# Weighting gathered pixels with one broadcast product on VectorE after the scan

## The chip, the cores and the metric

The kernel runs on one core of one Trainium2 chip. The metric is the device time of one execution in microseconds. A core has five engines that run their own instruction queues in order and meet through semaphores: TensorE (PE), VectorE (DVE), ScalarE (ACT), GpSimd (POOL) and SyncE (SP). Sixteen DMA engines move data for all queues.

## The reference

The input x has 4 images of 96 channels and 64 x 64 pixels. Four layers follow each other, each added to its input. Layer 0 is a selective scan in four directions over 4096 pixels, with 192 channels of 16 states. Layer 1 is a deformable convolution, and the change is in it:

```python
offset = _conv(x, offset_w, offset_b)
mask = jax.nn.sigmoid(_conv(x, mask_w, mask_b))
...
for k in range(K * K):                       # nine taps
    py = base_y[None, :, None] + i * DIL + dy
    px = base_x[None, None, :] + j * DIL + dx
    samp = _bilinear(x, py, px) * mask[:, k][:, None]
    out = out + jnp.einsum('bchw,oc->bohw', samp, weight[:, :, i, j])
...
# _bilinear: the four pixels around (py, px), weighted
return (1 - wy_) * (1 - wx_) * v00 + (1 - wy_) * wx_ * v01 + wy_ * (1 - wx_) * v10 + wy_ * wx_ * v11
```

Each output pixel thus needs, for each of nine taps, four neighbouring pixels of 96 channels, each times one number, summed. Layer 2 is a spectral filter over the 4096 pixels (a Fourier transform, an elementwise complex step, the inverse) and a feed-forward net with quantised operands; layer 3 is linear attention and a second such net.

## The kernel before, in words

All matrices are spread over 128 partitions. The program is one long list of instructions whose order is made when the kernel is built: nothing is decided on the chip. Layer 0's scan (`Layer0.scan`) runs from near the start until about 7635 us. Two other streams of work are woven into it and go on behind it. The stream `ends` prepares layer 0's inputs for all images and then computes layers 2 and 3 of image 0, 1, 2, 3, one after the other; image b waits until `net.sampled` holds b. The stream `middle` finishes layer 0 for an image, and then does layer 1 for it (`Layer1.image`), image after image.

Both streams are Python generators that yield planned costs. `Clock` keeps, for PE, DVE, ACT and POOL, when each would be free by these costs, and a step is emitted when the engines that it needs are planned to be free within some microseconds (`AHEAD`) and its data are ready. `pipe` keeps several chains of a kind in flight (eight for the sampling), limited by the buffers that they take. A yield's `cost(dve=..., act=...)` is such a plan: it says where the instructions stand in each engine's queue, not how long they take. Once the scan is over, `alone` steps the two streams in turn, and `net.own_banks` is set: the PSUM banks that the scan had are then given to `ends`.

Layer 1 of an image first writes a table in DRAM, in which one row holds a pixel and its three neighbours, 4 x 96 numbers. `positions` computes for every output pixel and tap a row number (`idx`) and four weights with the mask in them (`wt`, 128 partitions x 288 x 4). `sample` then works on blocks of 128 output pixels, t = 0 to 31, and three taps at a time (k0 = 0, 3, 6): 96 triples for an image. For a triple, `taps` does this:

- L1301: three indirect DMAs issued by POOL gather 128 rows each into the tile `g`, 128 x 3 x 384; six such tiles are in turn.
- L1312: twelve ACT activations multiply each group of 96 channels by its weight, one number per partition.
- L1318 and L1319, where `added` holds (`net.own_banks` is set): DVE sums the four corners to one in two adds of 128 x 576 and 128 x 288.
- L1331: PE transposes what is left into PSUM, three matmuls in that case and twelve that accumulate otherwise; L1339: ACT copies to the tile `st`.
- After six triples (two blocks of 128 pixels), L1347: nine matmuls of the convolution, and L1352: DVE adds bias and residual, SP stores (L1354).

In the layers 2 and 3 of the other stream the lines named later are these: L1466 and L1474 the first layer and its scaling on DVE, L1425 with the ACT copy L1434 the transforms by 64, L1491 with the activation L1492 the transform with twiddles, L1505, L1507, L1510 and L1512 the way back with the sum on DVE, L471, L487, L512 the norms, L1637 and L1639 the attention's products.

`added` is true for the sampling of image 3 alone: images 0 to 2 are sampled while the scan runs.

Of the kernel before, what the change touches and what calls it, by code (L numbers as in the profile page):

```python
# [19 lines left out]
B, C, H, W = 4, 96, 64, 64  # L20
# [163 lines left out]
def cost(pe=0.0, dve=0.0, act=0.0, pool=0.0, **more):  # L184
    return Step((pe, dve, act, pool), **more)


def wait(us=0.0, **more):

    return Step((0.0,) * 4, us, **more)  # L190
# [82 lines left out]
def pipe(net, chains, width, every=0, **tiles):  # L273


    chains, active = iter(chains), []
    clock, known, more = net.clock, net.known, True
    end, free = clock.now(), tiles
    while True:
        if more and len(active) < width:  # L280
            steps = next(chains, None)
            if steps is None:
                more = False
            else:
                active.append(Chain(steps, clock.now()))
                continue
        if not active:
            break
        for n, chain in enumerate(active):
            if chain.new and not net.has_bank():  # L290
                continue
            if any(a.done <= chain.done + every for a in active[:n]):
                continue
            if not all(free[tag] > 0 for tag in chain.takes):
                continue
            if clock.has_room(known.get((chain.kind, chain.done), (1.0,) * 4), chain.ready):
                break
        else:
            yield BLOCKED
            continue  # L300
        for tag in chain.takes:
            free[tag] -= 1
        clock.precede(known.get((chain.kind, chain.done), (0.0,) * 4))
        step = next(chain.steps, None)
        if step is None:
            net.hold(-chain.holds)
            active.remove(chain)
            end = max(end, chain.ready)
            continue
        for tag in step.frees:  # L310
            free[tag] += 1
        known[chain.kind, chain.done] = step.work
        chain.ready = clock.queue(step, chain.ready)
        chain.done += 1
        net.hold(step.holds - chain.holds)
        chain.holds, chain.new, chain.takes = step.holds, step.new, step.takes
        yield None
    yield wait(max(0.0, end - clock.now()))
# [796 lines left out]
class Layer1:  # L1115
# [168 lines left out]
    def sample(self, b, idx, wt):  # L1284
        net = self.net
        tc, nc = net.tc, net.nc
        with tc.tile_pool(name=f"l1g{b}", bufs=1, side="right") as gp:
            wdc = gp.tile([C, 9, 128], F32, name=f"wdc{b}", tag="wdc")
            nc.sync.dma_start(wdc, net.ins["wdc"])
            sts = {}  # L1290

            def taps(t, k0):

                yield wait(takes="g")
                key = f"{b}_{t}_{k0}"
                j, q = divmod(t, 2)
                cs = slice(j * 256, (j + 1) * 256)
                g = gp.tile([128, 3, 4 * C], F32, name=f"g{key}", tag="g", bufs=6)
                for k in range(3):
                    n = 9 * t + k0 + k  # L1300
                    nc.gpsimd.indirect_dma_start(  # L1301
                        out=g[:, k, :],
                        out_offset=None,
                        in_=self.tables[b % 2],
                        in_offset=bass.IndirectOffsetOnAxis(ap=idx[:, n : n + 1], axis=0),
                    )
                    yield cost(pool=1.5, wait=7.0 * (k == 2))
                for k in range(3):
                    for c in range(4):
                        pixel = g[:, k, c * C : (c + 1) * C]  # L1310
                        n = 9 * t + k0 + k
                        nc.scalar.activation(pixel, pixel, AF.Identity, scale=wt[:, n, c : c + 1])  # L1312
                    if k < 2:
                        yield cost(act=0.7)
                added = net.own_banks is not None
                if added:

                    nc.vector.tensor_add(g[:, :, : 2 * C], g[:, :, : 2 * C], g[:, :, 2 * C :])  # L1318
                    nc.vector.tensor_add(g[:, :, :C], g[:, :, :C], g[:, :, C : 2 * C])  # L1319
                first = q == 0 and k0 == 0  # L1320
                yield cost(dve=1.0 * added, act=0.7, new=True, takes="st" if first else "")
                if first:
                    sts[j] = gp.tile([C, 9, 256], F32, name=f"st{b}_{j}", tag="st")
                st = sts[j]


                corners = 1 if added else 4
                pt = net.mm(f"ps{key}", C)[:, : 3 * 128].rearrange("p (k t) -> p k t", t=128)
                for k in range(3):
                    for c in range(corners):  # L1330
                        nc.tensor.matmul(  # L1331
                            pt[:, k, :],
                            lhsT=g[:, k, c * C : (c + 1) * C],
                            rhs=net.ident,
                            is_transpose=True,
                            start=(c == 0),
                            stop=(c == corners - 1),
                        )
                nc.scalar.copy(st[:, k0 : k0 + 3, 128 * q : 128 * q + 128], pt)  # L1339
                yield cost(pe=0.4 if added else 1.3, act=0.5, new=True, frees="g")  # L1340
                if q == 0 or k0 < 6:
                    return
                xr = gp.tile([C, 256], F32, name=f"xr1_{b}_{j}", tag="xr")
                nc.sync.dma_start(xr, self.x1[b][:, cs])
                po = net.mm(f"pd{b}_{j}")[:, :256]
                for k in range(9):
                    nc.tensor.matmul(po, lhsT=wdc[:, k, :], rhs=st[:, k, :], start=(k == 0), stop=(k == 8))  # L1347
                    if k % 3 == 2:
                        last = k == 8
                        yield cost(pe=1.4, holds=1, takes="xo" if last else "", frees="st" if last else "")  # L1350
                xo = gp.tile([C, 256], F32, name=f"xo1_{b}_{j}", tag="xo")
                nc.vector.scalar_tensor_tensor(xo, po[:C], net.vec(V_L1B, C), xr, ALU.add, ALU.add)  # L1352
                yield cost(dve=0.5)
                nc.sync.dma_start(self.x2[b][:, cs], xo)  # L1354
                yield wait(frees="xo")

            chains = (taps(t, k0) for t in range(4 * NCH) for k0 in (0, 3, 6))
            yield from pipe(self.net, chains, 8, g=6, st=1, xo=1)

# [429 lines left out]
```

## Time and profile before

| what | value |
|---|---|
| time, median of three runs | 9014.61 us (9012.24 to 9038.34) |
| span of the profiled execution | 8965.3 us |
| median less that span, what lies around it | 49.3 us |
| busy: PE, DVE, ACT, POOL | 6639.1, 6689.3, 5244.1, 5561.5 us |
| activations at L1312 | 4608, of which 1152 for image 3 |
| adds at L1318 | 96, from 7867.9 to 8423.1 us |

The page gives the profiled execution's span, from its first to its last instruction, and no time around it; the runs' times include what lies before and after, so the two differ by the third row. Busy times overlap, since the engines work side by side. A group's line gives its source line, engine, operation, the tiles written and read and their shapes, the count, busy time in us and mean duration in ns, and then how long the engine was idle just before, with what ended the idling. Where the instructions of one group overlap, the busy time is less than the count times the mean. A wait's line says who waited for whom, for how long in total, how often, and the longest.

### The profile page before, as it was taken

How to read it: one execution, taken by the hardware profiler on the slowest of the kernel's cores; microseconds unless marked ns; L12 is line 12 of the kernel's file. 1: busy time of each engine (PE TensorE's matmuls, PEld its weight loads, DVE VectorE, ACT ScalarE, POOL GpSimd, SP SyncE). 2: the span in 40 equal slices, each digit the busy share in tenths (PEclk: the TensorE clock that was granted, in tenths of full speed). 3: DMA queues.
4: the chain of work that ended last, by engine and by line, in shares of the span. 5: the costliest groups of instructions: out<-in, count | busy, mean ns of one | idle time of the engine just before them, and what ended most of it. 6: DMA issues, size and time to landing. Idle time of an engine off the chain costs nothing.

```text
span 8965.3 us, 97776 instructions
## 1 busy us (share of the span) xinstructions
PE 6639.1 (74%) x31960; PEld 2926.8 (33%) x31960; DVE 6689.3 (75%) x4995; ACT 5244.1 (58%) x10214; POOL 5561.5 (62%) x4307
## 2 busy tenths in 40 slices
PE   6675967687767678777667888776888777766687
PEld 2111311122222233312223554122455322454373
DVE  0498889987889987788898887898887889223414
ACT  4564656555567767755566665545666665267623
POOL 0365657666668888766688887667888876245200
PEclk8776977798778889877778888787898887867798
DMA  1476777767778888877788888667888876434120
GB/s 51 133 205 173 193 191 220 198 183 181 189 202 231 235 224 228 204 199 194 200 230 219 233 218 213 160 177 193 215 229 222 216 188 156 104 108 131 57 62 12
DMA packets 776001, 1608.49 MB, mean 179 GB/s; under 512 B 247810, under 2 KB 339358, under 8 KB 773383
## 3 DMA queue, kind: packets, MB, share of 16 engines
q10 hardware_dynamic: 244224, 843.17, 36.4%
q1 hardware_dynamic: 457542, 532.51, 22.0%
q0 software_dynamic: 73728, 226.57, 9.6%
q8 instruction: 257, 4.21, 0.2%
q14 instruction: 250, 2.04, 0.1%
HBM read 1345.62 MB, written 256.29 MB: 179 GB/s over the span
## 4 chain that ended last, share of the span: by engine, by line
PE 35%; DVE 27%; DMA 15%; ACT 10%; issue 7%; POOL 2%; SPq 2%; ACTq 1%; another core or an unknown queue 0%; DVEq 0%; POOLq 0%
DVE hh L960 13%; DVE db L952 7%; DMA du<-du 5%; PE pc L691 4%; PE py L988 4%; ACT g L1312 4%; PE ps L1331 3%; PE db L938 3%; PE f L1425 3%; DMA da<-de 2%; PE pd L1347 2%; POOL hh L969 1%; DMA bc<-bcd 1%; ACT da L932 1%; PE h L1466 1%
## 5 line engine op out<-in xcount | busy, mean ns | idle before, releaser
L969 POOL TENSOR_TENSOR hh<-hh,bc 128x1024 f32<-128x1024 f32 x1536 | 3658.6, 2384 | 351.9 <-DVE hh L960 244.2
L960 DVE TENSOR_TENSOR_SCAN hh<-da,st,db 128x1024 f32<-128x1024 f32 x1152 | 2701.1, 2345 | 229.9 <-PE py L988 86.1
L952 DVE TENSOR_TENSOR db<-db,bc 128x1024 f32<-128x1024 f32 x1536 | 1863.4, 1213 | 523.2 <-PE db L938 517.9
L932 ACT ACTIVATE da<-da,w_al 128x1024 f32<-128x1024 f32 x1536 | 1741.5, 1146 | 641.0 <-DMA da<-de 287.2
L938 PE MATMUL db<-du,rep 96*128 96x512 bf16 x3072 | 1101.2, 447 | 824.6 <-DVE hh L960 764.5
L1301 POOL DMA_INDIRECT g<-table,idx x1152 | 1151.2, 999 | 546.3 <-issue 195.7
L1312 ACT ACTIVATE g<-g,wt 128x96 f32<-128x96 f32 x4608 | 1282.6, 365 | 146.8 <-DMA du<-du 37.3
L988 PE MATMUL py<-hh,w_fold 128*32 128x512 f32 x6144 | 1055.2, 760 | 24.2 <-POOL hh L969 10.7
L960 DVE TENSOR_TENSOR_SCAN hh<-da,db 128x1024 f32<-128x1024 f32 x384 | 877.3, 2285 | 71.9 <-PE py L988 22.1
L1331 PE MATMUL ps<-w_ident,g 128*96 128x128 f32 x3744 | 682.8, 322 | 300.6 <-ACT g L1312 142.7
L938 PEld LDWEIGHTS <-rep 96*128 96x128 bf16 x3072 | 284.3, 107 | 1772.3 <-issue 1139.0
L780 POOL TENSOR_TENSOR lw<-lw,w 128x512 f32<-128x512 f32 x192 | 244.3, 1273 | 820.9 <-DVE w L778 808.7
L1331 PEld LDWEIGHTS ps<-w_ident,g 128*96 128x96 f32 x3744 | 483.2, 142 | 655.0 <-ACT g L1312 255.2
L967 POOL COPY st<-hh 128x1 f32<-128x1 f32 x1152 | 233.3, 202 | 696.0 <-DVE hh L960 637.4
L691 PE MATMUL pc<-pad,wc 96*128 96x512 f32 x1152 | 548.4, 616 | 53.4 <-DMA wc<-wc_d 46.8
L1339 ACT COPY st<-ps 96x384 f32<-96x384 f32 x384 | 180.2, 472 | 395.5 <-PE ps L1331 301.6
L801 PE MATMUL pr<-ex,w_ident 128*128 128x512 f32 x384 | 281.5, 823 | 173.0 <-DVE ex L791 89.8
L778 DVE SCALAR_TENSOR_TENSOR w<-w,ex 128x512 f32<-128x512 f32 x192 | 159.4, 830 | 285.7 <-ACT w L775 285.6
L1318 DVE TENSOR_TENSOR g<-g 128x576 f32<-128x576 f32 x96 | 72.9, 759 | 390.0 <-ACT g L1312 360.5
L691 PEld LDWEIGHTS pc<-pad,wc 96*128 96x128 f32 x1152 | 217.1, 195 | 336.4 <-issue 305.3
L988 PEld LDWEIGHTS py<-hh,w_fold 128*32 128x32 f32 x6144 | 153.9, 122 | 511.0 <-issue 384.4
L769 PE MATMUL pd<-xd,w_dtw 103*64 103x512 f32 (+1 forms) x512 | 267.1, 800 | 66.5 <-DVE rl L782 27.5
(249 smaller groups left out, 8899.5 us busy)
## 6 DMA issues: line engine op xcount, KB each, us to landing
da<-de ACTq DMA_DIRECT2D x1536, 512.0 KB
du<-du SPq DMA_DIRECT2D x512, 192.0 KB
bc<-bcd SPq DMA_DIRECT2D x128, 512.0 KB
du<-du SPq DMA_DIRECT2D x128, 384.0 KB
y<-yb SPq DMA_DIRECT2D x384, 128.0 KB
de<-rl SPq DMA_DIRECT2D x128, 256.0 KB
m<-in_dft SPq DMA_DIRECT2D x128, 256.0 KB
ad<-y ACTq DMA_DIRECT2D x192, 128.0 KB
```

Of the source, the lines that this page charges most:

```text
L691: nc.tensor.matmul(pp, lhsT=wc[:, q, g * 128 : (g + 1) * 128], rhs=pad[:, r0 + dy : r0 + dy + NR, dx : dx + W], start=(q == 0), stop=(q == 8),
L801: nc.tensor.matmul(pr, lhsT=net.ident, rhs=ex, start=True, stop=False)
L932: self.net.nc.scalar.activation(u.da, u.da, AF.Exp, scale=self.al[:, a : a + 1])
L938: self.net.nc.tensor.matmul(db[:, h, :], lhsT=self.rep[:96, u.s % 4, :], rhs=u.du[u.s // 4][:, h * CH : (h + 1) * CH], start=True, stop=True,)
L952: self.net.nc.vector.tensor_mul(u.db, u.db, u.bc[:, 0, :])
L960: nc.vector.tensor_tensor_scan(u.along(u.hh), u.along(u.da), u.along(u.db), first, ALU.mult, ALU.add)
L969: self.net.nc.gpsimd.tensor_mul(u.hh, u.hh, u.bc[:, 1, :])
L988: nc.tensor.matmul(py[p0 : p0 + 32], lhsT=self.fold[:, u.i, :], rhs=hc[:, h * CH : (h + 1) * CH], start=u.sums["add"] is None and u.i == 0 ...
L1301: nc.gpsimd.indirect_dma_start(out=g[:, k, :], out_offset=None, in_=self.tables[b % 2], in_offset=bass.IndirectOffsetOnAxis(ap=idx[:, n : ...
L1312: nc.scalar.activation(pixel, pixel, AF.Identity, scale=wt[:, n, c : c + 1])
L1331: nc.tensor.matmul(pt[:, k, :], lhsT=g[:, k, c * C : (c + 1) * C], rhs=net.ident, is_transpose=True, start=(c == 0), stop=(c == corners - 1),)
L1425: nc.tensor.matmul(pt[64 * part : 64 * part + 64, c, :], lhsT=d[:, :, c0 + c], rhs=matrix[:, 64 * part : 64 * part + 64], start=True, stop ...
```

## The change

Where `added` holds, the twelve activations of a triple are left out. In their place DVE multiplies the whole tile `g`, 128 x 1152, by the weights, each of which is read for 96 channels by a stride of zero. The two adds follow it on the same engine. The test for `added` moves up. The planned costs change with it: ACT's three steps of 0.7 us per triple go (two of them were yields of their own), and the DVE step's 1.0 us becomes 2.6. For the images 0 to 2 the instructions are as before.

```diff
-                for k in range(3):
+                added = net.own_banks is not None
+                for k in range(0 if added else 3):
                     for c in range(4):
                         pixel = g[:, k, c * C : (c + 1) * C]
                         n = 9 * t + k0 + k
                         nc.scalar.activation(pixel, pixel, AF.Identity, scale=wt[:, n, c : c + 1])
                     if k < 2:
                         yield cost(act=0.7)
-                added = net.own_banks is not None
                 if added:
 
+                    weights = wt[:, 9 * t + k0 : 9 * t + k0 + 3, :].unsqueeze(3).to_broadcast([128, 3, 4, C])
+                    pixels = g.rearrange("p k (c d) -> p k c d", c=4)
+                    nc.vector.tensor_mul(pixels, pixels, weights)
                     nc.vector.tensor_add(g[:, :, : 2 * C], g[:, :, : 2 * C], g[:, :, 2 * C :])
                     nc.vector.tensor_add(g[:, :, :C], g[:, :, :C], g[:, :, C : 2 * C])
                 first = q == 0 and k0 == 0
-                yield cost(dve=1.0 * added, act=0.7, new=True, takes="st" if first else "")
+                yield cost(dve=2.6 * added, act=0.7 * (not added), new=True, takes="st" if first else "")
```

## The prediction

> **What bounds the kernel now.** The branch taken with `added` runs only once the bank pool of the scan is closed, so I began with the last instruction of the scan (L960, which starts for the last time at 7634.6 us) and asked for everything behind it by stretch. The columns are busy us and instruction counts, then granted clock and DMA.
>
> ```profile
> core 0: us, PE busy (x) PEld busy (x) DVE busy (x) ACT busy (x) POOL busy (x), PEclk, DMA share, GB/s
> 7834.00:8425.00 591.00, 389.49 (x2415) 282.16 (x2414) 188.23 (x319) 417.20 (x1395) 280.64 (x283) 0.69 0.39 113
> 8425.00:8515.00 90.00, 65.11 (x210) 29.32 (x208) 41.90 (x77) 33.49 (x73) 3.83 (x1) 0.82 0.03 8
> 8515.00:8965.00 450.00, 360.41 (x3028) 254.60 (x3028) 127.25 (x217) 137.26 (x270) 3.83 (x1) 0.90 0.12 38
> ```
>
> The first row is the sampling of image 3 beside layers 2 and 3 of image 2. The second is the rest of image 2, the third image 3 alone, on a busy PE. Nothing before 7834 can move: images 0 to 2 are sampled by the old branch. So 681 us, from 7834 to 8515, are at stake; the third row follows whatever ends last before it. ACT is the busiest engine of the first row, with 417.2 of 591. The groups of that stretch on ACT, and the waits of DVE and POOL in it, say with what:
>
> ```profile
> L1312 ACT ACTIVATE g<-g,wt 128x96 f32<-128x96 f32 x1152 | 318.7, 367 | 0.0
> ...
> DVE g L1318 <- ACT g L1312: 360.5, 82, 42.1
> ...
> DVE g L1318 <- DMA g<-table,idx: 1.9, 2, 1.7
> ...
> POOL g L1301 <- ACT st L1339: 84.6, 22, 21.9
> POOL g L1301 <- issue: 81.0, 203, 9.4
> POOL g L1301 <- ACT g L1312: 69.6, 24, 11.6
> ```
>
> The weighting is 318.7 of ACT's 417.2 us. DVE, whose queue is in order, stands 360.5 us at the head of its first add until ACT has weighted the pixels, 3.75 us per triple, with image 2's DVE work behind it; almost never (1.9 us) does it wait for a gather. POOL waits for buffers that ACT frees late. The chain of waits over the same stretch gives the share that decides:
>
> ```profile
> by line: ACT g L1312 29.4%; issue 11.5%; PE pd L1347 8.1%; PE f L1425 7.6%; another core or an unknown queue 6.4%; PE ps L1331 6.2%; PE yp L1505 3.3%; PE h L1466 3.1%; PE o L1510 2.5%; ACT st L1339 2.1%; DVE g L1318 2.1%; PE zp L1491 1.8%;
> ```
>
> 29.4% of 591 us is 174 us in which the chain runs through these activations. One triple in the timeline, late in the stretch:
>
> ```profile
> 8386.31 3.29 ACT L1312 ACTIVATE g<-g,wt 128x96 f32<-128x96 f32 x12
> ...
> 8389.64 0.76 DVE L1318 TENSOR_TENSOR g<-g 128x576 f32<-128x576 f32 x1 [4.83 <-ACT g L1312]
> 8390.43 0.46 DVE L1319 TENSOR_TENSOR g<-g 128x288 f32<-128x288 f32 x1
> ```
>
> Twelve activations take 3.29 us, DVE idles 4.83 us for them, and its own two adds take 1.2 us.
>
> **What the Trainium skill says.** "VectorE: DVE Perf Modes", section on the TRN2 errata, gives an fp32 tensor_tensor of N elements (N+151)/0.96 ns: 757 ns at 576 and 457 ns at 288. The trace agrees, with medians of 758 and 458. "ScalarE: Activation LUTs", section "What ACT_TABLE_LOAD costs", gives 186 + 0.833 N ns, 93 more for a pointer operand and 93 of overlap back to back: 359 ns and one each 266 ns. The trace shows a median of 363 and 318.7/1152 = 277 ns apart. "SBUF — State Buffer", "Who interferes with whom", says that a DVE instruction with two SBUF inputs contends with a GpSimd one that reads SBUF. The gather at 8034.98 took 1.40 us beside an add, against 0.94 alone.
>
> **The change, part by part.**
>
> Removed: 96 triples x 12 = 1152 activations, 318.7 us of ACT. ACT keeps 417.2 - 318.7 = 99 us, the copies. ACT's chain part goes too: 174 us.
>
> Added: 96 products of 1152 elements. By the two adds' rows the slope is (758 - 458)/288 = 1.04 ns an element and the rest 158 ns, so 1.36 us each; the page's form gives 1357 ns, and the one broadcast product in the trace, L572 with 2304 elements, took 2.555 us, the same slope. The stride-zero innermost weight is not in the trace. Lower bound: 1.2 us, the slope alone. Upper bound: the strided product L785, 1.084 us for 512 elements, 1.8 ns an element, which makes 2.2 us. I take 1.36: DVE gets 131 us more, and goes from 188 to 319 of the stretch. With the high value it is 211 more and 399.
>
> On the chain each triple's 3.29 us becomes 1.36 us, a part of 0.41. 174 x 0.41 = 72 us stay, **102 us go**. With 2.2 us it would be 58. If the new product were wholly covered, 174 would go.
>
> The planner's prices: ACT loses 3 x 0.7 = 2.1 planned us per triple, DVE gets 1.6 (1.0 to 2.6), and two steps of a chain vanish. POOL stays at 3 x 1.5 = 4.5 us per triple, the largest price, so the gathers' pace in the plan should hold, while layer 2's chains (PE, then an ACT copy) find an emptier ACT queue and are placed earlier among the triples. Some of the 90 us of image 2 behind the sampling then moves beside it. Bounds: 0 and 90; also below zero, if DVE's fuller queue pushes layer 2's DVE steps back, at most its 71 us of DVE work in the stretch (188 - 96 x 1.22). I take 18 us of gain.
>
> The wait: the product needs all three gathers landed, where ACT began with the first tap. Behind it in DVE's queue stand the two adds, the outputs L1352 (and their stores on SP's queue), and layer 2's scaling and sums (L1474, L1512), for which PE waits. I cost this at nothing because the data lie ready: the last gather was issued at 8395.23 and its triple's activations begin at 8419.3, 24 us later. The cover is ACT's lateness, which the change removes; the rival below prices that. No DMA is moved or added. POOL is slowed where its gather meets a product: the adds' 117 us of DVE cost it 280.6 - 3.5 - 282 x 0.94 = 12 us, so the product adds some 14 us, against 281 us in which POOL idles.
>
> PE's 389 us stay; image 2's rest needs PE too. After the change PE is the next bound, then POOL: 288 gathers, 1.25 us from start to start when nothing holds them, make 360 us.
>
> Sum: 102 + 18 = **120 us** off the span, 8965.3 to 8845. The median of the three runs is 9014.6, 49.3 above the profiled span, which I take as unchanged around it: **8895 us**. Own range of this case: 8835 to 8965.
>
> **The rivals.**
>
> *Layer 2 catches up fully.* Image 2 ends with the sampling, and image 3 starts at once. PE would need 389 + 65 = 454 us, POOL 360 + 14. At 454/470, 97% of PE, the stretch from 7834 ends at 8304 instead of 8515: 211 us, 8804. For it: ACT at 99 us is out of the way. Against it: PE was at most 80% busy even with image 3 alone (360/450).
>
> *Gathers crowd out the other queues.* When 18 gathers ran without a gap, from 8027.4 to 8050.3, PE was only half busy, and ACT stood 6.0 us for a "remote" cause behind it; in the burst from 8347 to 8366 ACT stood 10.5 us. If gathers are no longer held by late buffers, such bursts become the rule. The PE work of the stretch at one half during 360 us of gathers is 180, the other 274 us at 90% take 305: 665 against 681, 16 us, 8998. Against it: gathers come in threes as buffers fall free, and in most bursts of six PE stayed over 70% busy.
>
> *DVE stands for the gathers: slower.* The product is at the head of DVE's queue before its third tap has landed; a landing took about 3 us on the three occasions when the chain of waits passed through one (3.05, 3.02 and 2.69 us). Today a triple occupies or holds DVE 3.75 + 1.22 us, later w + 1.36 + 1.22, so it decides at **w = 2.4 us** a triple. A product that reaches the head as its gathers are being issued waits up to 3 x 1.25 + 3 = 6.7 us. With w = 4 DVE loses 1.6 x 96 = 154 us, and with half of it on the path the span grows by 77: 9092. For it: layer 2's sums and scalings share the queue. Against it: 1.9 us of such waits now, and the plan allows 7 us behind the third gather.
>
> *It doesn't do what it says.* If `added` held for other images too, 384 products would meet the scan, where DVE is over 80% busy in most slices of the page. The condition is the bank pool, which is set after the scan; the 96 adds at L1318 start at 7867.9, so I give this no share.
>
> **How the numbers follow.** The main case 0.60; layer 2 catching up 0.18; crowding 0.10; DVE standing 0.12. A difference under 0.3%, 27 us, is no more than the runs' own scatter (9012 to 9038), so the crowding case counts as the same. Of the main case nearly all lies beyond 27 us: 0.78 faster, 0.10 same, 0.12 slower. The likeliest is 8895. The range reaches to 8775, below the catching-up case with PE a little quicker, and to 9010, over the crowding case; outside are the standing case and a sliver below.
>
> **What would show it.** Right: L1312 has 3456 activations, not 4608, and a 128x1152 product has 96 at 1.3 to 1.45 us; ACT's busy time after the scan falls by about 319 us; the sum L1318 no longer waits for ACT, and the product's wait for the gathers stays below 2.4 us each; the stretch from the first gather of image 3 to the last activation copy shrinks from 591 to some 490 us; image 3 alone still takes 445 to 450. Wrong: the product at 2 us or more, over 230 us of DVE waits on gathers, gathers in long runs with PE half idle, or an image 2 that ends more than 90 us behind the sampling.

## The result, and the profile after

| | before | after |
|---|---|---|
| median of six runs each | 9013.42 us (8959.19 to 9038.34) | 8906.1 us (8875.78 to 8930.03) |
| span of the profiled execution | 8965.3 us | 8877.9 us |

The ratio is 0.9891, with a 95% interval of 0.9867 to 0.9916: the changed kernel is faster, by about 98 us (76 to 120 by the interval; the two medians differ by 107). Two later comparisons, each on a chip of its own, gave 0.9874 and 0.9884. The medians differ between chips (the kernel before took 8933 to 8940 us on the later ones), so everything below is compared as a ratio to the kernel before on the same chip; a ratio r is worth (r - 1) x 8935 us there.

All lines of the changed source below the edit are three further down: L1318 became L1321, L1331 L1334, L1339 L1342, L1347 L1350, L1425 L1428. The activation is L1313, the product L1320.

First the busy times by stretch, for the kernel after, cut as before: the sampling of image 3, the rest of image 2, image 3 alone. The columns are the stretch, its length, then busy us and instructions of each engine, granted clock, DMA share and rate.

```profile
core 0: us, PE busy (x) PEld busy (x) DVE busy (x) ACT busy (x) POOL busy (x), PEclk, DMA share, GB/s
7858.00:8368.00 510.00, 397.30 (x2638) 283.65 (x2637) 325.68 (x433) 136.37 (x285) 346.79 (x289) 0.80 0.46 135
8368.00:8409.00 41.00, 24.87 (x69) 9.13 (x67) 30.15 (x60) 16.58 (x32) 3.83 (x1) 0.63 0.04 13
8409.00:8878.00 469.00, 377.06 (x3028) 265.33 (x3028) 127.16 (x217) 137.18 (x270) 3.83 (x1) 0.85 0.12 37
```

The first two rows took 681 us before and take 551 now (the cuts are rounded by up to 8 us; the table of the experiments counts from single instructions). ACT fell from 417 to 136 us in the sampling (copies of image 2 moved in beside it), DVE rose from 188 to 326, and POOL from 281 to 347, although it issues the same 288 gathers (the cut before leaves out six of them). The third row did not follow: 469 us instead of 450, to which the section on the hardware comes back. On exact cuts the first two rows fell by 137 us and the span by only 87, since in this pair the first gather of image 3 also came 32 us later (at 7858.3 instead of 7826.6 us), behind instructions that the change does not touch.

The groups behind these sums, of the kernel after in the same stretch, and the activation's group from the page:

```profile
L1301 POOL DMA_INDIRECT g<-table,idx x288 | 343.3, 1192 | 217.7 <-DVE wt L1281 71.7 <-issue 69.0 <-PE ps L1334 62.4
L1320 DVE TENSOR_TENSOR g<-g,wt 128x1152 f32<-128x1152 f32 x96 | 129.8, 1352 | 91.8 <-DMA g<-table,idx 79.2 <-issue 12.6
```

```profile
L1313 ACT ACTIVATE g<-g,wt 128x96 f32<-128x96 f32 x3456 | 963.9, 364 | 167.6 <-DMA du<-du 52.2
```

The edit is there as announced: 3456 activations and 96 products of 1352 ns. A gather now takes 1192 ns in the mean, where it took 982. The waits of the stretch:

```profile
ACT st L1342 <- PE ps L1334: 135.8, 52, 13.9
DVE g L1320 <- DMA g<-table,idx: 79.2, 36, 13.9
...
POOL g L1301 <- issue: 69.0, 227, 0.3
POOL g L1301 <- PE ps L1334: 62.4, 12, 20.5
```

ACT, which all waited for, now waits for PE. DVE's 360.5 us of waiting for ACT are gone, and 79.2 us of waiting for gathers stand in their place. POOL waits 0.3 us at most between two gathers in 227 cases of 288: it issues them in long runs, and its longer pauses (62.4 us in 12 cases) are for tiles that the transposes L1334 empty. The chain of waits over the stretch no longer has a dominant line:

```profile
by line: PE f L1428 15.8%; issue 14.2%; PE pd L1350 8.2%; PE ps L1334 5.5%; DMA g<-table,idx 5.3%; DVE g L1320 4.9%; PE h L1469 4.6%; PE yp L1508 4.1%; POOL g L1301 3.8%; PE o L1513 3.1%; DVE g L1321 2.9%; PE pk L1640 2.8%; PE pa L1644 2.7%
```

How the three engines interlock is best seen in two triples of the timeline, start and duration in us, with PE, ACT and the later adds left out:

```profile
8270.87 0.95 POOL L1301 DMA_INDIRECT g<-table,idx  x1 [0.31 <-issue]
...
8271.54 1.36 DVE L1320 TENSOR_TENSOR g<-g,wt 128x1152 f32<-128x1152 f32 x1 [1.80 <-DMA g<-table,idx]
...
8272.12 1.60 POOL L1301 DMA_INDIRECT g<-table,idx  x1 [0.30 <-issue]
...
8272.94 0.76 DVE L1321 TENSOR_TENSOR g<-g 128x576 f32<-128x576 f32 x1
...
8274.03 0.98 POOL L1301 DMA_INDIRECT g<-table,idx  x1 [0.30 <-PE pk L1640]
...
8275.31 0.95 POOL L1301 DMA_INDIRECT g<-table,idx  x1 [0.30 <-issue]
...
8275.94 1.36 DVE L1320 TENSOR_TENSOR g<-g,wt 128x1152 f32<-128x1152 f32 x1 [1.75 <-DMA g<-table,idx]
...
8276.56 1.55 POOL L1301 DMA_INDIRECT g<-table,idx  x1 [0.30 <-issue]
```

In each of these triples one gather begins while the product runs, and that gather takes 1.55 to 1.60 us instead of 0.95; the first one ends 0.02 us after the add that follows the product (8273.72 and 8273.70). A triple takes 4.4 us from product to product, which is POOL's own pace: 0.98 + 0.95 + 1.55 and three pauses of 0.30. In such a burst DVE stands 1.8 us for the gathers, but it stands there because it is faster than POOL.

### The profile page after: what moved, and what is told of

Read it like the earlier page. It is cut to its first block, busy times and chain, and to the rows that moved or that the text cites. A ratio compares the mean times of both kernels' runs of the same rounds, so it can differ in the third digit from the quotient of the medians.

```text
span 8877.9 us, 96298 instructions
## 1 busy us (share of the span) xinstructions
PE 6652.4 (75%) x31960; PEld 2922.8 (33%) x31960; DVE 6807.1 (77%) x5091; ACT 4943.6 (56%) x9062; POOL 5620.9 (63%) x4307
## 4 chain that ended last, share of the span: by engine, by line
PE 35%; DVE 28%; DMA 16%; ACT 8%; issue 8%; POOL 3%; SPq 2%; ACTq 1%; DVEq 0%; another core or an unknown queue 0%; POOLq 0%
DVE hh L960 14%; DVE db L952 7%; DMA du<-du 6%; PE pc L691 4%; PE py L988 4%; PE f L1428 3%; PE db L938 3%; PE ps L1334 3%; DMA da<-de 2%; ACT g L1313 2%; PE pd L1350 2%; POOL hh L969 1%; ACT da L932 1%; PE h L1469 1%; PE py L983 1%
## 5 line engine op out<-in xcount | busy, mean ns | idle before, releaser
L1301 POOL DMA_INDIRECT g<-table,idx x1152 | 1210.6, 1051 | 407.2 <-issue 176.0
L1313 ACT ACTIVATE g<-g,wt 128x96 f32<-128x96 f32 x3456 | 963.9, 364 | 167.6 <-DMA du<-du 52.2
L1334 PE MATMUL ps<-w_ident,g 128*96 128x128 f32 x3744 | 675.3, 320 | 215.0 <-ACT g L1313 138.0
L1334 PEld LDWEIGHTS ps<-w_ident,g 128*96 128x96 f32 x3744 | 480.1, 141 | 569.4 <-ACT g L1313 249.6
L691 PE MATMUL pc<-pad,wc 96*128 96x512 f32 x1152 | 547.8, 615 | 53.4 <-DMA wc<-wc_d 46.3
L1342 ACT COPY st<-ps 96x384 f32<-96x384 f32 x384 | 179.7, 472 | 458.2 <-PE ps L1334 350.6
L1350 PE MATMUL pd<-st,wdc 96*128 96x256 f32 x1152 | 302.4, 411 | 7.8 <-ACT st L1342 4.1
```

Source lines behind the costliest of these rows:

```text
L691: nc.tensor.matmul(pp, lhsT=wc[:, q, g * 128 : (g + 1) * 128], rhs=pad[:, r0 + dy : r0 + dy + NR, dx : dx + W], start=(q == 0), stop=(q == 8),
L1301: nc.gpsimd.indirect_dma_start(out=g[:, k, :], out_offset=None, in_=self.tables[b % 2], in_offset=bass.IndirectOffsetOnAxis(ap=idx[:, n : ...
L1334: nc.tensor.matmul(pt[:, k, :], lhsT=g[:, k, c * C : (c + 1) * C], rhs=net.ident, is_transpose=True, start=(c == 0), stop=(c == corners - 1),)
```

## The experiments

The table gives the stretch that matters in each kernel's profile: from the first gather of image 3 to the store of image 2's output (sampling plus the rest). The times of single profiles in it scatter: the kernel before took 686.1 and 641.1 us, the kernel after 549.0, 521.9 and 523.0. Part of that has a name in the views, though no explanation: in the first trace of each kernel ACT and DVE have waits for a "remote" cause (on ACT 45.4 us before, 79.0 after; 38 and 8 us of the chain of waits), and none of the twelve later traces has any in this stretch. So the ratios decide, and the traces of before again and after again are the better pair.

| kernel | ratio to before, 95% | sampling + rest of image 2 | gathers of image 3, mean ns | image 3 alone |
|---|---|---|---|---|
| before, first trace | 1 | 686.1 | 982 | 444.5 |
| after, first trace | 0.9891 [0.9867, 0.9916] | 549.0 | 1192 | 462.4 |
| order of after, ACT weights (e1) | 1.0124 [1.0103, 1.0145] | 728.1 | 983 | 446.8 |
| product, order of before (e2) | 0.987 [0.9851, 0.9889] | 529.5 | 1149 | 447.0 |
| a second product (e3) | 0.9911 [0.9888, 0.9934] | 557.3 | 1223 | 446.5 |
| a memset (e4) | 0.9913 [0.9896, 0.993] | 552.1 | 1304 | 448.2 |
| before again | one run, 8927.55 us | 641.1 | 988 | 450.3 |
| after again | 0.9874 [0.9854, 0.9895] | 521.9 | 1183 | 450.0 |
| cheaper gathers in the plan (e7) | 0.987 [0.9846, 0.9895] | 520.7 | 1186 | 462.6 |
| a third of the convolution (e8) | 0.9867 [0.9843, 0.989] | 488.1 | 1191 | 465.3 |
| after, third run | 0.9884 [0.9867, 0.9901] | 523.0 | 1193 | 443.9 |
| two memsets (e11) | 0.9956 [0.994, 0.9973] | 591.3 | 1338 | 466.9 |
| a reduction (e12) | 0.9924 [0.9906, 0.9942] | 565.6 | 1056 | 460.4 |
| one tap on ACT (e6) | 0.9892 [0.9876, 0.9909] | 522.9 | 1092 | 443.8 |

The first two rows are the comparison above. The rows from e1 to e4 ran on one chip, those from before again to e8 on another, and the last four on a third.

### Was it the engine, or the order of the instructions?

The change does two things: it moves work from ACT to DVE, and it changes the planned costs, so that the planner writes another order of everything in that stretch. Each was made alone. All diffs in this part are against the kernel after. The first keeps the order of after, and ACT does the weighting:

```diff
-                for k in range(0 if added else 3):
+                for k in range(3):
...
-                    if k < 2:
+                    if k < 2 and not added:
...
-                    weights = wt[:, 9 * t + k0 : 9 * t + k0 + 3, :].unsqueeze(3).to_broadcast([128, 3, 4, C])
-                    pixels = g.rearrange("p k (c d) -> p k c d", c=4)
-                    nc.vector.tensor_mul(pixels, pixels, weights)
```

> The twelve ACT activations of each triple as in the kernel before, but emitted in one step and priced as in the changed kernel, so that the order of all other instructions is the changed kernel's. Theory A (the gain is ACT's work leaving the chain): no gain, 8990 to 9030 us. Rival B (the gain is the new order that the planner's prices make): most of it is here, 8905 to 8935. If both count, between.

It is slower than before: 1.0124, some 110 us, which neither theory had. Apart from the weighting, its trace has the instructions of after on DVE, ACT and POOL, in the same order. Its chain of waits, and its largest wait, over the sampling:

```profile
by line: ACT g L1313 33.5%; PE pd L1347 9.2%; issue 8.4%; PE ps L1331 6.9%; PE f L1425 4.7%; DMA g<-table,idx 3.8%; PE yp L1505 3.1%; PE o L1510 2.4%; DVE g L1318 2.2%; PE pk L1637 2.0%; PE lncf L471 1.8%; PE pa L1641 1.7%; POOL g L1301 1.7
```

```profile
DVE g L1318 <- ACT g L1313: 450.9, 91, 23.2
```

33.5% of 688 us is 230 us of activations on the chain, against 174 in the first trace of before and 199 in before again (36.0% of 552). The new order by itself gains nothing; with the weighting on ACT it costs.

The second has the product and the order of before:

```diff
-                for k in range(0 if added else 3):
-                    for c in range(4):
+                for k in range(3):
+                    for c in range(0 if added else 4):
...
-                yield cost(dve=2.6 * added, act=0.7 * (not added), new=True, takes="st" if first else "")
+                yield cost(dve=1.0 * added, act=0.7, new=True, takes="st" if first else "")
```

> The DVE product of the changed kernel, with the steps and prices of the kernel before, so that the order of all other instructions is the kernel before's. Theory A: 70 to 100 us of gain, 8915 to 8945; what is missing to the changed kernel is the order's part, image 2's tail. Rival B: 8990 to 9015, no gain to speak of.

It has the whole gain: 0.987, some 116 us, more than the 70 to 100 expected, and its trace has the order of before. Its stretches:

```profile
7821.00:8254.00 433.00, 338.61 (x2480) 256.74 (x2479) 315.21 (x415) 120.15 (x245) 334.14 (x289) 0.83 0.54 159
8254.00:8350.00 96.00, 73.02 (x210) 36.96 (x208) 41.63 (x77) 33.38 (x73) 3.83 (x1) 0.75 0.01 1
8350.00:8797.00 447.00, 359.58 (x3028) 254.07 (x3028) 127.21 (x218) 136.97 (x270) 3.83 (x1) 0.90 0.12 36
```

The sampling is shorter than after the change and the rest of image 2 longer (96 instead of 41 us), with the sum the same within the scatter. So the order moves image 2's work from behind the sampling to beside it, as predicted, but it is paid for there. That the gain comes from moving the weighting to DVE is shown; a gain from the order is not seen (0.987 here, 0.9874, 0.9884 and 0.9891 for after, with overlapping intervals).

To set the traces of before and after beside each other on one chip, both were run again:

> The kernel before unchanged, for its stages on the same chip as the runs beside it: from the end of the scan to the first gather of image 3 190 us, sampling 599, the rest of image 2 87, image 3 alone 445.

> The changed kernel unchanged, for its stages on the same chip: 0.988 to 0.991 of the kernel before; sampling about 510 us and the rest of image 2 about 40. If the 18 us that image 3 lost in the first profile came from a clock that was granted late and by chance, image 3 alone takes 445 to 448 here; if the change does it, 462 again.

The sum of sampling and rest went from 641.1 to 521.9 us, 119 less: 70 of it in the sampling and 50 in the rest. Before again is a single execution; after again, timed, gave 0.9874, about 113 us. The whole stretch in both, before again first:

```profile
7826.15:8467.25 641.10, 450.50 (x2692) 311.54 (x2690) 229.92 (x396) 451.27 (x1469) 292.02 (x290) 0.73 0.37 108
7843.39:8365.30 521.91, 424.82 (x2700) 299.42 (x2698) 355.67 (x492) 153.13 (x317) 347.96 (x290) 0.79 0.45 132
```

PE has the same matmuls in both (a few records are missing), does them in 26 us less at a higher granted clock (0.79 against 0.73), and pauses 97 us instead of 191. In the chain of waits PE's lines together hold 311 of the 522 us, where they held 241 of 641. So part of the gain comes with PE's clock; whether the shorter pauses raised it, or something else did, is not shown. The same kernel ran a third time, on the last chip, for the comparisons there:

> The changed kernel unchanged, as the base on this chip: 0.987 to 0.990 of the kernel before, gathers of image 3 at a mean of 1.18 to 1.19 us, sampling 480 to 510 us.

It gave 0.9884, about 104 us.

### What holds the stretch now?

First the price that the planner puts on a gather, since 1.5 us was above what a gather took:

```diff
-                    yield cost(pool=1.5, wait=7.0 * (k == 2))
+                    yield cost(pool=1.25 if net.own_banks else 1.5, wait=7.0 * (k == 2))
```

> The changed kernel with the planned price of a gather lowered from 1.5 to 1.25 us after the scan, so that triples are placed closer together among image 2's work. Theory E (what is left is set by the order): the sampling shrinks from 510 to 440 to 470 us, image 2's rest grows from 40 to 70 to 95, and the sum is 5 to 20 us less, ratio 0.985 to 0.989. Theory F (PE's work sets the sum, whatever the order): the sum stays within 5 us, ratio 0.989.

Nothing changed, as theory F has it: 0.987 against 0.9874, and 520.7 us for the stretch against 521.9 (474.4 for the sampling and 46.3 for the rest). Then PE, which was to be the next bound, was relieved of six of nine convolution matmuls for image 3, so that six taps are left out:

```diff
-                    nc.tensor.matmul(po, lhsT=wdc[:, k, :], rhs=st[:, k, :], start=(k == 0), stop=(k == 8))
+                    if k % 3 == 2 or not added:
+                        nc.tensor.matmul(po, lhsT=wdc[:, k, :], rhs=st[:, k, :], start=(k == (2 if added else 0)), stop=(k == 8))
```

> The changed kernel in its own order, with three of the nine matmuls of the convolution for image 3 (the other six taps left out): 16 x 6 x 2 records, some 49 us of PE less. Theory F (PE sets the stretch after the change): 35 to 50 us less, ratio 0.984 to 0.986. If gathers on POOL set it, under 10 us less, ratio 0.988 to 0.990.

In the profile the stretch fell by 34 us, to 488.1, with PE busy 52 us less. But image 3 alone was 15 us longer in it, and the timed runs, 0.9867 against 0.9874, are 6 us apart, where theory F asked for 35 to 50 and the intervals carry no difference. PE's part is thus suggested and not settled.

### What does DVE's time cost, and what the stretched gathers?

If DVE's time were free, more of it beside the sampling would cost nothing; if the gathers set the pace, only work that stretches them would cost. A second product on 768 elements (952 ns), and in its place a memset of as many, which reads nothing:

```diff
+                    more = gp.tile([128, 2, 4, C], F32, name=f"more{key}", tag="more", bufs=1)
+                    nc.vector.tensor_mul(more, pixels[:, :2], weights[:, :2])
                     nc.vector.tensor_mul(pixels, pixels, weights)
```

> The changed kernel with a second, unpriced product of 128x768 into a tile that nothing reads, ahead of each product: 96 x 0.96 = 92 us more of DVE, with two SBUF inputs. Theory C (gathers are the pace, and two-input DVE instructions stretch them): gathers grow from a mean of 1.19 to about 1.35 us, 8945 to 8975 in all, clearly slower than the memset's kernel. Rival D (DVE's own time is the pace): 8940 to 8990, and the memset's kernel the same. If DVE and POOL both have slack: 8906.

```diff
+                    more = gp.tile([128, 2, 4, C], F32, name=f"more{key}", tag="more", bufs=1)
+                    nc.vector.memset(more, 0.0)
                     nc.vector.tensor_mul(pixels, pixels, weights)
```

> As the kernel with the second product, but what is added is a memset of 128x768, of about the same DVE time and without an SBUF input. Theory C: gathers stay at 1.19 us, 8906 to 8925. Rival D: 8940 to 8990, like the second product.

The pair did not tell the two apart: 0.9911 and 0.9913. As ratios to the first comparison's 9013 us, the ranges were 0.992 to 0.996 (C) and 0.992 to 0.997 (D) for the second product, and 0.988 to 0.990 (C) and again 0.992 to 0.997 (D) for the memset; neither kernel fell in any of them. The memset was no control. It was cheaper than meant (698 ns, 67 us in all, where the second product added 91), and the gathers were longer in its kernel, not shorter: 1304 ns against 1223. After itself did not run on that chip; against the ratios of after elsewhere both are some 25 us slower. So two memsets, and a reduction of the pixels to one number each partition, which reads one input and writes next to nothing:

```diff
+                    more = gp.tile([128, 2, 4, C], F32, name=f"more{key}", tag="more", bufs=1)
+                    nc.vector.memset(more, 0.0)
+                    nc.vector.memset(more, 0.0)
                     nc.vector.tensor_mul(pixels, pixels, weights)
```

> The changed kernel with two unpriced memsets of 128x768 ahead of each product, into a tile that nothing reads: 96 x 1.29 = 124 us more of DVE. One such memset lengthened the gathers from 1.19 to 1.30 us. Theory C (gathers are the pace and DVE instructions stretch them): gathers at about 1.42 us, 66 us more of POOL, 40 to 65 us slower than the changed kernel, ratio 0.992 to 0.996. Rival D (DVE's own time): as slow as the kernel with the reduction. Neither: within 10 us of the changed kernel.

```diff
+                    more = gp.tile([128, 1], F32, name=f"more{key}", tag="more", bufs=1)
+                    nc.vector.reduce_sum(more, g, axis=mybir.AxisListType.XY)
                     nc.vector.tensor_mul(pixels, pixels, weights)
```

> The changed kernel with one unpriced reduction of the gathered 128x1152 to 128x1 ahead of each product: about 1.35 us each, 130 us more of DVE, one SBUF input, next to nothing written. Theory C: gathers stay near 1.19 us and the time within 15 us of the changed kernel. Rival D (DVE's own time is the pace): 50 to 100 us slower, ratio 0.993 to 0.999.

Both add about the same time to DVE, 134 and 129 us. Two memsets cost (0.9956 - 0.9884) x 8933 = 64 us, the reduction (0.9924 - 0.9884) x 8933 = 36 us, each uncertain by some 20 us by the intervals. The groups of DVE over the whole program, then those of POOL over the sampling, the two memsets first and the reduction below:

```profile
L1321 DVE MEMSET more<- 128x768 f32 x96 | 67.0, 698 | 10.6 <-DVE wt L1281 0.2 <-issue 0.2
L1322 DVE MEMSET more<- 128x768 f32 x96 | 67.0, 698 | 21.8 <-DVE more L1321 20.4 <-DMA g<-table,idx 1.4
```

```profile
L1301 POOL DMA_INDIRECT g<-table,idx x284 | 381.4, 1343 | 139.4 <-PE ps L1337 60.0 <-issue 58.6 <-DVE g L1324 9.4
```

```profile
L1321 DVE TENSOR_REDUCE more<-g 128x1 f32<-128x1152 f32 x96 | 129.0, 1344 | 39.4 <-DMA g<-table,idx 39.3
```

```profile
L1301 POOL DMA_INDIRECT g<-table,idx x281 | 297.4, 1059 | 190.9 <-PE ps L1336 94.0 <-issue 63.8 <-DVE g L1324 12.3
```

Beside the reduction the gathers were even shorter than in after (89 of the 288 began inside a reduction and kept their 945 ns), and 36 us were lost all the same: there POOL waits for buffers (94.0 us for L1336, the transposes that empty them, against 39.0 in after's third run). So DVE's time costs even where it stretches no gather, some 0.28 us for each us added; but the reduction also holds the tile g for 1.34 us longer, and the run does not separate the two. The memsets cost 28 us more, a difference uncertain by some 20 us too, with POOL's gathers 42 us longer than in after (385.3 against 343.6 over all 288). Neither the gathers alone nor DVE alone explains both runs. That the second 28 us are due to the gathers is the likeliest reading, and not more: the two kernels differ in what DVE does in other ways too.

The last one takes a third of the product back to ACT, which has time to spare now:

```diff
-                for k in range(0 if added else 3):
+                for k in range(1 if added else 3):
...
-                    if k < 2:
+                    if k < 2 and not added:
...
-                    weights = wt[:, 9 * t + k0 : 9 * t + k0 + 3, :].unsqueeze(3).to_broadcast([128, 3, 4, C])
-                    pixels = g.rearrange("p k (c d) -> p k c d", c=4)
+                    weights = wt[:, 9 * t + k0 + 1 : 9 * t + k0 + 3, :].unsqueeze(3).to_broadcast([128, 2, 4, C])
+                    pixels = g[:, 1:3].rearrange("p k (c d) -> p k c d", c=4)
...
-                yield cost(dve=2.6 * added, act=0.7 * (not added), new=True, takes="st" if first else "")
+                yield cost(dve=2.2 * added, act=1.1 if added else 0.7, new=True, takes="st" if first else "")
```

> The changed kernel with the first tap of each triple weighted by four ACT activations and a product of 128x768 for the other two: DVE 0.4 us less a triple, ACT 1.1 us more. Theory C: gathers 0.03 to 0.05 us shorter, 5 to 15 us faster than the changed kernel at best. If the hand-over from ACT to DVE counts as before the change, a third of the chain's share comes back: 20 to 35 us slower.

It equals after: 0.9892 against 0.9884, and 522.9 us against 523.0 (433.7 for the sampling and 89.2 for the rest, a split like e2's). DVE is relieved of 38 us and POOL of 29, and DVE's add waits 96.1 us for ACT:

```profile
L1321 DVE TENSOR_TENSOR g<-g 128x576 f32<-128x576 f32 x96 | 73.1, 761 | 100.3 <-ACT g L1313 96.1
```

That the two cancel is one way to read it, and that neither lies on the path another; the runs do not decide. After again, its third run, e2, e6 and e7 all lie between 520.7 and 529.5 us. Which engine sets that time is open. In after again PE is busy 401 of 483 us of the sampling, DVE 326, and POOL 344, with another 86 us in pauses of some 0.30 us, one behind each gather. PE is the fullest, and holds most of the chain. No version was faster than after by more than the intervals.

## Why the prediction was right, and where its steps were not

The predicted 120 us came out as 98, 113 and 104 in the three timed comparisons, whose intervals are 76 to 120, 94 to 131 and 88 to 119: it lies at the edge of the first, inside the second and just above the third. The direction, the engine and the size of the main term held; other terms of the working did not, and the main one came near in part by luck.

**The swap: 102 us predicted.** The product alone, in the old order, gave 116 us (99 to 133 by its interval). The price of 1.36 us per product, read from the two adds' slope, was met at 1352 ns, so the stride-zero weight costs nothing extra. The form in the Trainium skill, "VectorE: DVE Perf Modes", section on the TRN2 errata, gave 1357, and the trace agrees. The split of the chain was wrong, though. The product was to keep 72 us of it; it holds 25 in after (4.9% of 510), and 24 to 28 in e2, after again and the third run. The activations held 174 us in the one trace that the step was read from, but 199 in before again. So the chain lost some 150 to 175 us here, and other lines took part of that back, PE's above all (241 to 311 us from before again to after again). The sum has no term for this, and that the net came near 102 is in good part luck.

**The order: 18 us predicted as a gain.** This step failed. The rest of image 2 did shrink, by 48 us and not 18 (87.3 to 39.5), but as work moved into the sampling, where it is paid for: e2, without it, has the same sum. The error was to count the shorter tail as time saved, without asking what the sampling would have to take up for it. By e1 the order, with the weighting left on ACT, is a loss of 110 us. Without these 18 us the sum is 102, well inside all three intervals.

**PE: 389 us that stay.** The matmuls stayed and their time did not: over sampling and rest PE was busy 460.1 us before and 421.9 after in the first traces, and 450.5 and 424.8 in the second pair, at granted clocks of 0.71, 0.79, 0.73 and 0.79. The working had taken PE's speed as given.

**POOL: 14 us predicted.** The gathers of image 3 grew from 283 to 343 us, 60 us, four times as much. The step scaled what the adds had cost POOL per us of DVE time, when gathers came in short bursts and the meeting was a matter of chance. Now gathers run back to back, and in 76 of the 96 triples of the first trace one began while the product ran: those took 1551 ns in the mean, 0.6 us more each, which makes 46 of the 60 us. The rest is mostly gathers that began in image 2's DVE instructions, some of them right ahead of a product. The cover named, 281 us in which POOL idled, went as well: its pauses of 0.35 us and more between gathers fell from 217 us (167 in before again) to 65 (39 in after again). The Trainium skill, "SBUF — State Buffer", section "Who interferes with whom", has a rule that fits, a DVE instruction with two SBUF inputs against a GpSimd one that reads SBUF, and this trace shows 1.55 to 1.60 us against 0.95. So the floor of POOL was not 360 + 14 but 343 + 288 x 0.3 = 430 us. It did not decide here, since e6, whose gathers take 29 us less, is no faster.

**Layer 2 catches up.** The rival's stretch of 470 us did not come: after took 549.0, 521.9 and 523.0, and image 2 ended some 40 us behind the sampling each time. POOL's floor of 430 us alone would have left room for it.

**DVE's wait for the gathers: nothing predicted, 2.4 us a triple the point where it decides.** 79.2 us over 96 triples are 0.83 us, and 101.3 in after again are 1.06: far below. The slower rival did not happen. Where such waits come in rows, as in the timeline above, they are 1.8 us each, and POOL's pace sets them: DVE, at 2.6 us a triple, is ahead of POOL at 4.4.

**Gathers that crowd out the others.** They did come in long runs, as that rival said, but PE was busy 0.78 of the sampling in the first trace of after (397 of 510) and not one half. The "remote" waits on which the rival leaned are in the first traces alone; after again, with as many gathers in a row, has none.

**What lies around the span: 49.3 us predicted.** This was a misreading, without effect. The changed kernel's profiled execution took 8879.74 us at a span of 8877.9: 1.8 us lie around it, and before again shows the same (8927.55 and 8925.7). The 49.3 us were scatter between executions. Since they were added to both sides, the difference stood.

Of the signs named, the stretch to the last copy took 509.6, 482.4 and 483.5 us in three traces, with 490 predicted. ACT over the whole program fell by 300.5 us, from 5244.1 to 4943.6: the weighting's group by the full 318.7 (1282.6 to 963.9), while ACT's other work took 18 us more. Image 3 alone fell outside its 445 to 450 in the first trace of after, and not because of the change: DVE, ACT and POOL run image 3 alone in the same order before and after, and the other two traces of after took 450.0 and 443.9.

## What the runs showed of the hardware

**The clock of PE can stand at half for a stretch of identical instructions.** Image 3 alone took 443.8 to 466.9 us in these profiles. For the kernel after, the inverse transform L1508 in its first trace and again in the second, the same instructions:

```profile
8660.58 2.71 PE L1508 MATMUL yp<-i,d 128*96 128x64 f32 x16
```

```profile
8615.97 1.50 PE L1508 MATMUL yp<-i,d 128*96 128x64 f32 x16
```

The window around each shows the granted clock, in the third column from the right: 0.50 in the first, 1.00 in the second.

```profile
8655.00:8690.00 35.00, 30.47 (x125) 22.36 (x123) 8.80 (x7) 3.56 (x7) 0.00 (x0) 0.50 0.08 27
```

```profile
8612.00:8635.00 23.00, 17.91 (x128) 12.83 (x128) 8.86 (x7) 4.07 (x7) 0.00 (x0) 1.00 0.15 46
```

From the first to the last of eight such groups it took 35.3 us (8651.80 to 8687.11) instead of 22.3 (8609.58 to 8631.90): 13 us, about as much as the 12.4 us between 462.4 and 450.0 for image 3 alone in the two traces; in other places the first trace lost 5 us more and regained 6. The Trainium skill, "TensorE: Matmul & The Clock Gate", Part 1, says that the gate passes either half of the pulses or all, and that its window runs free of the kernel, so that the slow matmuls differ between runs; the values 0.50 and 1.00 agree. It also has the full clock come after one busy window of some 3.4 us. That does not fit here, where PE was busy 30 of 35 us and stayed at half; the measurement decides.

**A gather that begins inside a product lasts until the add behind the product is done.** In the first trace of after 76 gathers began while a product ran, and all 76 ended 0.02 to 0.03 us after the first add behind it; they took 0.95 to 2.16 us, by how early in the product they had begun. The 29 gathers that had begun on an idle DVE, and in which a product then began, kept 0.94 to 0.95 us.

The section of the Trainium skill on SBUF also says that a DVE instruction with at most one SBUF input does not contend on this chip, outside modes in which it uses both ports. For the reduction that held: 89 gathers began in one and took 945 ns in the mean.

```profile
8201.85 1.35 DVE L1321 TENSOR_REDUCE more<-g 128x1 f32<-128x1152 f32 x1
8202.56 0.94 POOL L1301 DMA_INDIRECT g<-table,idx  x1 [0.30 <-issue]
```

With memsets it depends on what follows. In the kernel with two of them a gather that began in one kept its length where a pause came behind that memset, and was held through the product and the first add where the product followed at once:

```profile
7857.55 0.70 DVE L1321 MEMSET more<- 128x768 f32 x1
7857.77 0.95 POOL L1301 DMA_INDIRECT g<-table,idx  x1 [0.30 <-issue]
...
7847.19 0.70 DVE L1322 MEMSET more<- 128x768 f32 x1 [0.23 <-DVE more L1321]
7847.28 2.64 POOL L1301 DMA_INDIRECT g<-table,idx  x1 [0.30 <-issue]
7847.81 1.29 DVE L1323 TENSOR_TENSOR g<-g,wt 128x1152 f32<-128x1152 f32 x1
7849.14 0.76 DVE L1324 TENSOR_TENSOR g<-g 128x576 f32<-128x576 f32 x1
```

Of 85 such gathers, 31 had a memset behind which the product did not begin at once: all took 0.94 to 1.02 us. In 54 the product began before the memset had ended: 49 of them took 2.11 to 2.70 us and 5 kept 0.95. So a memset by itself stretched no gather here; one right ahead of a product lengthened the time in which a gather can be caught, and the mean rose from 1.19 to 1.30 us with one memset per triple and to 1.34 with two. A gather that began in image 2's DVE work right ahead of a product could be caught too, as several were in after itself (2.29 to 3.43 us).

## What to carry to other kernels

Where the chain of waits runs a third of a stretch through one engine's small instructions, moving them to another engine pays by what the chain loses, even if the receiving engine is then far fuller; price the move by the chain's share, read in more than one execution (174 and 199 us here), and expect other lines to take up part of what is freed. A shorter tail that comes from reordering is no gain until the stretch that took up the work is shown not to have grown: separate order from engine by building each alone. A price for two engines disturbing each other, read where one of them is mostly idle, does not hold once both run without a pause: count the meetings.
